# Moving a kernel's key weights and sigmoid weights to other byte offsets in SBUF

## The chip, the core and the metric

The kernel runs on one core of one Trainium2 chip. The metric is device time in microseconds (us), from start to end of one execution. A core has a matrix engine (TensorE; PE in the profile, with its weight loads listed apart as PEld), a vector engine (VectorE, DVE), an activation engine (ScalarE, ACT), a general engine (GpSimd, POOL) and a queue from which all transfers of this kernel start (SP). They run side by side and wait for each other through semaphores. SBUF is the on-chip memory: 128 partitions, each a row of bytes. A tile takes the same byte range in all of them, so a tile has one start address. PSUM is the small memory into which TensorE adds.

## The reference, cut to what matters

The input is x, 256 tokens of 512 numbers, and a context of 25,088 rows of 512. Three layers follow, each added to x. Only the first is touched by the change, and it is most of the work:

```
q = layernorm(x) @ Wq.T + bq            # 256 x 128
k = ctx @ Wk.T + bk                     # 25088 x 128
v = ctx @ Wv.T + bv                     # 25088 x 512
z = sigmoid(q @ k.T / sqrt(128))        # 256 x 25088
x = x + z @ v
```

Then come a causal attention with 16 heads over the 256 tokens, and eight experts of which each token uses one.

## The kernel before, in words

The context is cut into 49 chunks (NCH) of 512 rows (CK). Each chunk is loaded twice, once with the model dimension on the partitions (`rT`) and once with the rows on them (`rN`). Wv isn't applied to the chunks: the kernel adds up z @ ctx in two PSUM banks (`acc`) and applies Wv once at the end.

Products need nearly float32 accuracy. TensorE has a float32r form[...]. So each operand is split into a rounded high part, which ACT writes, and the remainder, a low part, which VectorE or GpSimd computes (`split`, L64 and L65). A product is three matmuls, high by high (L68), high by low (L69) and low by high (L70), all in `mm3`. The first operand is the stationary one (the weights: 128 columns of 4 bytes, 512 bytes in a partition); the second is the moving one (512 columns, 2048 bytes, in most cases). Each matmul has its own weight load, which runs while the matmul ahead of it is streaming.

For a chunk c the loop (it begins at line 263) does:

- `kp_mm`: the key projection. The weights are the four 128-column blocks j of `wk` (high and low tile), the moving data the four blocks of the split, transposed chunk (`T`). 12 matmuls of 512 columns add into one bank; `kp_out` adds bk and splits the keys again (`kp`).
- `scores`: for each half p of the chunk, 6 matmuls of 256 columns; the weights are 128 keys of `kp`, the moving data the split queries `qp`. ACT takes the sigmoid into `z`, VectorE adds it to `zacc` (line 189, for the bias of v), and a split writes the pair `zz[c, p]`. There are four buffers for each part of the pair.
- `av`: the weighted sum. The weights are 128x128 pieces of `zz`, the moving data the four blocks of the split chunk (`N`); for each of two groups of 128 queries 12 matmuls of 512 columns.
- `prepare`: side work that loads other weights, splits them and stores them back to HBM for the last part.

The order of all work on TensorE, ACT, VectorE and GpSimd is the order in which the program is written; `in_order` pins it at the end. Transfers go out in program order on SP.

Addresses come from two pools. The pool `sm` holds small tiles one after another, in the order in which the program first names them, each in a slot rounded up to 32 bytes. The pool `sb` follows it with the large tiles, all of which are multiples of 512 bytes long. A tile with several buffers takes as many slots. `sm` starts at 128 bytes modulo 512. `half`, of which only one column is used, is declared 41 columns wide, and `sb` starts at 0 modulo 512. So the blocks of `wk`, `T`, `kp`, `qp`, `zz` and `N` all start at 0 modulo 512.

At the start, `wk` is split in one piece (ACT and GpSimd); behind it on GpSimd stand the power for the two layer norms (`moments`, L129) and the split of wq. The tiles of `wk` are used again in the last part, as `fr` and `fq` of the experts.

Of the kernel before, what the change touches and what calls it, by code (L numbers as in the profile page):

```python
# [11 lines left out]
F32 = mybir.dt.float32  # L12
F32R = mybir.dt.float32r
BF16 = mybir.dt.bfloat16
# [6 lines left out]
P = 128  # L21
T = 256
D = 512
KD = D // P
# [4 lines left out]
E = 8  # L29
NH = 16  # L30
LAG = 2
# [17 lines left out]
def body(ctx, tc, a, out, nch=NCH):  # L49
    nc = tc.nc  # L50
# [3 lines left out]
    sm = ctx.enter_context(tc.tile_pool(name="sm", bufs=1))  # L54
    sb = ctx.enter_context(tc.tile_pool(name="sb", bufs=1))
# [3 lines left out]
    def f(t):  # L59
        return t.bitcast(F32)  # L60

    def split(hi, lo, src, eng=nc.vector):

        copy(hi, src)  # L64
        eng.tensor_tensor(lo, src, f(hi), ALU.subtract)  # L65

    def mm3(ps, ahi, alo, bhi, blo, first, last):
        mm(ps, lhsT=ahi, rhs=bhi, start=first, stop=False)  # L68
        mm(ps, lhsT=ahi, rhs=blo, start=False, stop=False)  # L69
        mm(ps, lhsT=alo, rhs=bhi, start=False, stop=last)  # L70

    def pair(name, shape, tag=None, bufs=1):
        return [sb.tile(shape, F32R, tag=f"{tag or name}{i}", name=f"{name}_{i}", bufs=bufs) for i in range(2)]

    def bank(name):
        return psum.tile([P, D], F32, tag="b", name=name, bufs=6)
# [4 lines left out]
    def toks(t):  # L81
        return slice(t * P, (t + 1) * P)


    ident = sm.tile([P, P], F32, name="ident")
    make_identity(nc, ident)
    half = sm.tile([P, 41], F32, name="half")[:, 0:1]
    nc.gpsimd.memset(half, -0.5)
    ones = sm.tile([P, 1], F32, name="ones")
    nc.gpsimd.memset(ones, 1.0)  # L90
    x_sb = [sb.tile([P, D], F32, tag=f"x{t}", name=f"x_sb{t}") for t in range(2)]
    bq = sm.tile([P, 1], F32, name="bq")
    bk = sm.tile([P, 1], F32, name="bk")
    bv = sb.tile([P, D], F32, name="bv")
    rows = sm.tile([P, 2], F32, name="rows")
    zacc = sb.tile([P, 2, T], F32, name="zacc")
    nc.vector.memset(zacc, 0.0)
    wv = pair("wv", [P, KD * D], "wvo")
# [1 line left out]


    plain = {"wkvd": D, "wqr": 4 * 64, "wkr": 64, "wku": D, "wvu": D, "wq2": KD * D, "gate": KD * E}
    pw = {n: (sb if w % P == 0 else sm).tile([P, w], F32, name=n) for n, w in plain.items()}
    plain = list(pw)
    spill = {n: dram.tile([P, 2 * w], F32, name=f"sp_{n}") for n, w in (("wo", KD * D), ("gu", E * 2 * D), ("dn", E * D))}

    todo = [("wv", at, None, at) for at in range(0, KD * D, D)]
# [2 lines left out]
    todo += [("wo", at, KD * D, at) for at in range(0, KD * D, D)]  # L110


    mask = sm.tile([P, P], BF16, name="mask")
    nc.gpsimd.memset(mask, 0.0)
    nc.gpsimd.affine_select(out=mask, in_=mask, compare_op=ALU.is_ge, fill=MASKED, base=0, pattern=[[-1, P]],
                            channel_multiplier=1)
# [5 lines left out]
    def moments(x, tag):  # L122
        s6 = sm.tile([P, nc.vector.BN_STATS_DIM], F32, tag="s6", name=f"s6{tag}", bufs=2)
        mv = sm.tile([P, 2], F32, tag="mv", name=f"mv{tag}", bufs=2)
        rs = sm.tile([P, 1], F32, tag="rs", name=f"rs{tag}", bufs=2)
        nc.vector.bn_stats(s6, x)
        nc.vector.bn_aggr(mv, s6)
        nc.vector.tensor_scalar(rs, mv[:, 1:2], 1e-5, None, ALU.add)
        nc.gpsimd.tensor_tensor(rs, rs, half, ALU.pow)  # L129
        return mv, rs  # L130
# [12 lines left out]
    rT, rN, sT, sN, kp, zz = {}, {}, {}, {}, {}, {}  # L143
# [24 lines left out]
    def kp_mm(c, blocks=range(KD)):  # L168
        th, tl = sT[c]
        if c not in kp:  # L170
            kp[c] = bank(f"kp_ps{c}")
        ps = kp[c]
        for j in blocks:
            mm3(ps, wk[0][:, toks(j)], wk[1][:, toks(j)], th[:, j, :], tl[:, j, :], j == 0, j == KD - 1)

    def kp_out(c):
        ps, kp[c] = kp[c], pair(f"kp{c}", [P, CK], "kp", 2)
# [3 lines left out]
    def scores(c, p):  # L181
        ps = bank(f"sc{c}_{p}").rearrange("p (i t) -> p i t", i=2)
        for i in range(2):
            t = toks(2 * p + i)
            mm3(ps[:, i, :], kp[c][0][:, t], kp[c][1][:, t], qp[0], qp[1], True, True)
        z = sb.tile([P, 2, T], F32, tag="z", name=f"z{c}_{p}", bufs=2)
        nc.scalar.activation(z, ps, AF.Sigmoid, scale=1.0 / math.sqrt(128.0))  # L187
        zz[c, p] = pair(f"z{c}_{p}", [P, 2, T], "z", 2 * LAG)
        tt2(zacc, zacc, z, ALU.add)  # L189
        split(*zz[c, p], z)  # L190

# [20 lines left out]
    def load_split(n, tag):  # L212
        r = sb.tile([P, D], F32, tag="wr", name=f"{n}_r", bufs=2)
        nc.sync.dma_start(r, a[n])
        return r, pair(n, [P, D], tag)

    wk_r, wk = load_split("wk", "wk")
    for t in range(2):
        nc.sync.dma_start(x_sb[t], a["x"][:, t, :])
    wq_r, wq = load_split("wq", "at")  # L220
# [8 lines left out]

    acc = [psum.tile([P, D], F32, tag=f"acc{q}", name=f"acc{q}") for q in range(2)]  # L230
    xh, xl = pair("xa", [P, KD, T], "oh")
    warm = sm.tile([P, 1], F32, name="warm")
    nc.scalar.activation(warm, half, AF.Sigmoid)
    split(*wk, wk_r, nc.gpsimd)
    m = [moments(x_sb[tt], f"a{tt}") for tt in range(2)]
    xn = [normal(x_sb[tt], m[tt], f"xa{tt}") for tt in range(2)]
    split(*wq, wq_r, nc.gpsimd)
# [1 line left out]
    for j in range(2):  # L239
        split_T(0, [j])  # L240
        split(xh[:, :, toks(j)], xl[:, :, toks(j)], xps[j])
    split_T(0, [2, 3], nc.gpsimd)
    kp_mm(0, [0, 1])
    qp = pair("qp", [P, T])
    ps = bank("qp_ps")[:, :T]
    for j in range(KD):
        mm3(ps, wq[0][:, toks(j)], wq[1][:, toks(j)], xh[:, j, :], xl[:, j, :], j == 0, j == KD - 1)
    kp_mm(0, [2, 3])
    split_T(1, [0, 1])
    split_T(1, [2, 3], nc.gpsimd)  # L250
    nc.scalar.activation(qp[0], ps, AF.Identity, bias=bq)
    nc.vector.scalar_tensor_tensor(qp[1], ps, bq, f(qp[0]), ALU.add, ALU.subtract)
    kp_out(0)
    split_N(0, [0, 1])
    kp_mm(1, [0, 1])
    scores(0, 0)
    scores(0, 1)
    split_N(0, [2, 3])
    kp_mm(1, [2, 3])
# [3 lines left out]
    for c in range(nch):  # L263
# [23 lines left out]
        for t in range(NT):  # L287
            for q in now:
                av(c, t, q)
            if nx and t in (1, 2):  # L290
                scores(c + 1, t - 1)
        if c >= 4 and plain:
            n = plain.pop()
# [271 lines left out]
    ps = bank("rows_ps")  # L565
# [54 lines left out]
    Q(1, 2)  # L620
    Q(1, 3)
    ft = sb.tile([P, 2 * D], F32R, tag="wq2", name="ft").rearrange("p (n b e d) -> p n b e d", n=2, b=2, e=2)
    fr, fq = (sb.tile([P, 2, 2, P], F32, tag=f"wk{i}", name=f"f{i}") for i in range(2))
    yhl = pair("y", [P, KD, T], "oh")
    PV(0, 2)
    PV(0, 3)
# [144 lines left out]
```

## Time and profile before

| What | Value |
|---|---|
| Median of 2 runs | 585.6 us (585.15 to 586.05) |
| Profiled execution | 586.28 us, its span 584.5 us |
| TensorE matmuls | 570.6 us busy, 98% of the span, 3036 instructions |
| Weight loads | 481.7 us, 82% |
| VectorE, ACT, GpSimd | 79%, 68%, 4% |
| Granted TensorE clock | full |
| DMA | 144.94 MB, mean 248 GB/s |

The span runs from the first to the last instruction; the 1.8 us left over lie around it. "Busy" adds up instructions as the profile shows them. Matmuls are pipelined and overlap, so the mean duration of one (some 390 ns) is longer than the distance between the starts of two, and that distance is the pace. A row of the timeline gives start, length, engine, line, operation, what is written and read, sizes and count. A row of the groups gives count, total busy time, mean, and idle time of the engine ahead of it.

### The profile page before, as it was taken

The numbers are of one execution on the slowest core, as the hardware profiler recorded it, in microseconds if no ns is written. First come the engines' busy times: TensorE is split into PE (matmuls) and PEld (weight loads), VectorE is DVE, ScalarE is ACT, GpSimd is POOL, SyncE is SP. The second block draws the span as 40 slices with busy tenths as digits, with TensorE's granted clock in tenths as the row PEclk, the third lists the DMA queues.
The fourth block names the chain that finished last, engine by engine and source line by source line (L and its number), as shares of the span: only waits on it lengthen the run. The fifth ranks groups of instructions, "written<-read, shape, count | busy, mean of one in ns | idle before, by whom it ended". The sixth has DMA issues, their size and how long they took to land.

```text
span 584.5 us, 8061 instructions
## 1 busy us (share of the span) xinstructions
PE 570.6 (98%) x3036; PEld 481.7 (82%) x3036; DVE 459.7 (79%) x528; ACT 395.1 (68%) x512; POOL 21.1 (4%) x28
## 2 busy tenths in 40 slices
PE   4999999999999999999999999999999999999997
PEld 3888888888888888888888888888888887876996
DVE  6898888888888888888888888787878765667543
ACT  5877777777777777777777776767676752574211
POOL 5200000000000000000000000000000041000000
PEclk9999999999999999999999999999999999999999
DMA  8897887879888888788988887565657477700000
GB/s 288 334 368 283 278 295 281 321 278 317 287 324 276 325 271 325 266 337 298 332 282 319 274 337 245 208 225 206 234 198 243 149 295 262 316 1 1 1 1 36
DMA packets 33526, 144.94 MB, mean 248 GB/s; under 512 B 4240, under 2 KB 4432, under 8 KB 19792
## 3 DMA queue, kind: packets, MB, share of 16 engines
q1 hardware_dynamic: 33488, 144.44, 69.3%
q8 instruction: 23, 0.38, 0.2%
q14 instruction: 15, 0.12, 0.1%
HBM read 129.22 MB, written 15.20 MB: 247 GB/s over the span
## 4 chain that ended last, share of the span: by engine, by line
PE 95%; DVE 3%; DMA 1%; issue 0%; POOL 0%; ACT 0%; SPq 0%; POOLq 0%
PE acc L68 15%; PE acc L69 15%; PE acc L70 15%; PE kp_ps L70 8%; PE kp_ps L69 8%; PE kp_ps L68 8%; PE sc L70 4%; PE sc L69 4%; PE sc L68 4%; PE s L428 2%; PE gu L68 1%; PE gu L69 1%; PE gu L70 1%; PE pt L445 1%; DMA wq_r<-in_wq 1%; PE pv L456 1%
## 5 line engine op out<-in xcount | busy, mean ns | idle before, releaser
L68 PE MATMUL acc<-N,z 128*128 128x512 f32 x392 | 153.9, 393 | 0.0
L69 PE MATMUL acc<-N,z 128*128 128x512 f32 x392 | 153.7, 392 | 0.0
L65 DVE TENSOR_TENSOR N<-rN,N 128x2048 fp32r<-128x2048 f32 (+1 forms) x53 | 111.6, 2110 | 52.3 <-ACT N L64 52.2
L70 PE MATMUL acc<-N,z 128*128 128x512 f32 x392 | 152.5, 389 | 0.0
L65 DVE TENSOR_TENSOR T<-rT,T 128x2048 fp32r<-128x2048 f32 (+1 forms) x49 | 110.3, 2252 | 15.3 <-ACT T L64 15.3
L187 ACT ACTIVATE z<-sc 128x512 f32<-128x512 f32 x98 | 58.7, 599 | 66.5 <-PE sc L70 66.2
L64 ACT CAST N<-rN 128x2048 fp32r<-128x2048 f32 (+1 forms) x55 | 94.4, 1725 | 6.1
L64 ACT CAST T<-rT 128x2048 fp32r<-128x2048 f32 (+1 forms) x55 | 94.3, 1721 | 0.9 <-DMA rT<-in_ctxT 0.7
L70 PEld LDWEIGHTS acc<-N,z 128*128 128x128 f32 x392 | 73.6, 188 | 16.0
L68 PEld LDWEIGHTS acc<-N,z 128*128 128x128 f32 x392 | 74.0, 189 | 12.3
L69 PEld LDWEIGHTS acc<-N,z 128*128 128x128 f32 x392 | 74.0, 189 | 11.7
L68 PE MATMUL kp_ps<-T,wk 128*128 128x512 f32 x196 | 76.9, 392 | 0.0
L70 PE MATMUL kp_ps<-T,wk 128*128 128x512 f32 x196 | 76.7, 392 | 0.0
L69 PE MATMUL kp_ps<-T,wk 128*128 128x512 f32 x192 | 74.7, 389 | 0.0
L189 DVE TENSOR_TENSOR zacc<-zacc,z 128x512 f32<-128x512 f32 x98 | 67.2, 686 | 3.7 <-ACT z L187 1.7
L65 DVE TENSOR_TENSOR z<-z,z 128x512 fp32r<-128x512 f32 x98 | 67.3, 686 | 0.0
L64 ACT CAST z<-z 128x512 fp32r<-128x512 f32 x98 | 61.0, 623 | 3.1
L178 ACT ACTIVATE kp<-kp_ps,bk 128x512 fp32r<-128x512 f32 x49 | 33.9, 691 | 39.9 <-PE kp_ps L70 39.9
L70 PE MATMUL sc<-qp,kp 128*128 128x256 f32 x196 | 55.8, 285 | 0.1
L69 PE MATMUL sc<-qp,kp 128*128 128x256 f32 x196 | 55.4, 283 | 0.0
L68 PE MATMUL sc<-qp,kp 128*128 128x256 f32 x196 | 54.9, 280 | 0.0
L68 PEld LDWEIGHTS kp_ps<-T,wk 128*128 128x128 f32 x196 | 37.1, 189 | 7.8
(177 smaller groups left out, 658.5 us busy)
## 6 DMA issues: line engine op xcount, KB each, us to landing
rN<-in_ctxN SPq DMA_DIRECT2D x49, 1024.0 KB, 5.7
rT<-in_ctxT SPq DMA_DIRECT2D x47, 1024.0 KB, 5.5
sp_gu<-w_gu SPq DMA_DIRECT2D x32, 256.0 KB, 4.3
gu<-sp_gu SPq DMA_DIRECT2D x8, 1024.0 KB, 6.0
r_gu<-in_gu SPq DMA_DIRECT2D x16, 256.0 KB, 5.7
sp_dn<-w_dn SPq DMA_DIRECT2D x16, 256.0 KB, 4.3
dn<-sp_dn SPq DMA_DIRECT2D x16, 256.0 KB, 6.0
r_dn<-in_dn SPq DMA_DIRECT2D x8, 256.0 KB, 6.1
```

The costliest lines, as they stand in the source:

```text
L64: copy(hi, src)
L65: eng.tensor_tensor(lo, src, f(hi), ALU.subtract)
L68: mm(ps, lhsT=ahi, rhs=bhi, start=first, stop=False)
L69: mm(ps, lhsT=ahi, rhs=blo, start=False, stop=False)
L70: mm(ps, lhsT=alo, rhs=bhi, start=False, stop=last)
L178: nc.scalar.activation(kp[c][0], ps, AF.Identity, bias=bk)
L187: nc.scalar.activation(z, ps, AF.Sigmoid, scale=1.0 / math.sqrt(128.0))
L189: tt2(zacc, zacc, z, ALU.add)
L428: mm(p3[:, h - h0:h - h0 + 2, :], lhsT=qs[:, tt, h // 2, g, :], rhs=kbd[g // 2][:, g % 2, h:h + 2, :nk], start=tt == 1, stop=tt == 0 and h ...
L445: nc.tensor.transpose(ps[:, toks(i * (tt + 1) + kt)], pr[tt, u][:, i, toks(kt)], ident)
L456: mm(pv[tt][r, g, :], lhsT=vs[kt][:, g * P + r.start:g * P + r.stop], rhs=pt[tt, u][:, toks(i * (tt + 1) + kt)], start=kt == 0, stop=kt == tt)
```

## The change: what it does

`wk`'s two tiles move from `sb` to `sm` and become 16 columns longer. The four blocks are no longer adjacent: they begin at columns 1, 132, 264 and 400. The declarations of small tiles are reordered, `half` becomes 16 columns wide and a `pad` of 8 columns is added, so that both tiles of `wk` and the pool `sb` start at 32 modulo 512. The split of `wk` goes block by block: four casts and four subtractions in place of one each. Each buffer of `zz` becomes 16 columns (64 bytes) longer, of which the data use the first 512. `fr` and `fq` take their place in the longer `wk` tiles.

```
+    wkp = [None, None]
+    wkp[0] = sm.tile([P, D + 16], F32R, tag="wk0", name="wk0")
+    plain = {"wkr": 64, "gate": KD * E}
+    pw = {n: sm.tile([P, w], F32, name=n) for n, w in plain.items()}
+    half = sm.tile([P, 16], F32, name="half")[:, 0:1]
+    wkp[1] = sm.tile([P, D + 16], F32R, tag="wk1", name="wk1")
+    pad = sm.tile([P, 8], F32, name="pad")
     ident = sm.tile([P, P], F32, name="ident")
-    half = sm.tile([P, 41], F32, name="half")[:, 0:1]
...
-            mm3(ps, wk[0][:, toks(j)], wk[1][:, toks(j)], th[:, j, :], tl[:, j, :], j == 0, j == KD - 1)
+            mm3(ps, wk[0][j], wk[1][j], th[:, j, :], tl[:, j, :], j == 0, j == KD - 1)
...
-        zz[c, p] = pair(f"z{c}_{p}", [P, 2, T], "z", 2 * LAG)
+        zz[c, p] = [t[:, 0:2 * T].rearrange("p (i t) -> p i t", i=2)
+                    for t in pair(f"z{c}_{p}", [P, 2 * T + 16], "z", 2 * LAG)]
...
-    wk_r, wk = load_split("wk", "wk")
+    wk_r = sb.tile([P, D], F32, tag="wr", name="wk_r", bufs=2)
+    nc.sync.dma_start(wk_r, a["wk"])
+    wk = [[t[:, o:o + P] for o in (1, 132, 264, 400)] for t in wkp]
...
-    split(*wk, wk_r, nc.gpsimd)
+    for j in range(KD):
+        split(wk[0][j], wk[1][j], wk_r[:, toks(j)], nc.gpsimd)
...
-    fr, fq = (sb.tile([P, 2, 2, P], F32, tag=f"wk{i}", name=f"f{i}") for i in range(2))
+    fr, fq = (sm.tile([P, D + 16], F32, tag=f"wk{i}", name=f"f{i}")[:, 0:D].rearrange("p (b e d) -> p b e d", b=2, e=2)
+              for i in range(2))
```

More of the change, by code (lines that the diff above doesn't have):

```diff
@@ L82, in toks @@
         return slice(t * P, (t + 1) * P)
+    ones, bq, bk, warm = [sm.tile([P, 1], F32, name=n) for n in ("ones", "bq", "bk", "warm")]
+    rows = sm.tile([P, 2], F32, name="rows")
+    mask = sm.tile([P, P], BF16, name="mask")
+    wkp = [None, None]
[5 more added lines that the diff above has]
+    pad = sm.tile([P, 8], F32, name="pad")
     ident = sm.tile([P, P], F32, name="ident")
     make_identity(nc, ident)
-    half = sm.tile([P, 41], F32, name="half")[:, 0:1]
     nc.gpsimd.memset(half, -0.5)
-    ones = sm.tile([P, 1], F32, name="ones")
     nc.gpsimd.memset(ones, 1.0)
     x_sb = [sb.tile([P, D], F32, tag=f"x{t}", name=f"x_sb{t}") for t in range(2)]
-    bq = sm.tile([P, 1], F32, name="bq")
-    bk = sm.tile([P, 1], F32, name="bk")
     bv = sb.tile([P, D], F32, name="bv")
-    rows = sm.tile([P, 2], F32, name="rows")
     zacc = sb.tile([P, 2, T], F32, name="zacc")
@@ L102, in body @@
     plain = {"wkvd": D, "wqr": 4 * 64, "wkr": 64, "wku": D, "wvu": D, "wq2": KD * D, "gate": KD * E}
-    pw = {n: (sb if w % P == 0 else sm).tile([P, w], F32, name=n) for n, w in plain.items()}
-    plain = list(pw)
+    pw.update({n: (sb if w % P == 0 else sm).tile([P, w], F32, name=n) for n, w in plain.items() if n not in pw})
+    plain = list(plain)
     spill = {n: dram.tile([P, 2 * w], F32, name=f"sp_{n}") for n, w in (("wo", KD * D), ("gu", E * 2 * D), ("dn", E * D))}
@@ L110, in body @@
     todo += [("wo", at, KD * D, at) for at in range(0, KD * D, D)]
-    mask = sm.tile([P, P], BF16, name="mask")
     nc.gpsimd.memset(mask, 0.0)
@@ L231, in body @@
     xh, xl = pair("xa", [P, KD, T], "oh")
-    warm = sm.tile([P, 1], F32, name="warm")
     nc.scalar.activation(warm, half, AF.Sigmoid)
-    split(*wk, wk_r, nc.gpsimd)
+    for j in range(KD):
+        split(wk[0][j], wk[1][j], wk_r[:, toks(j)], nc.gpsimd)
     m = [moments(x_sb[tt], f"a{tt}") for tt in range(2)]
```

## The prediction

> **What bounds the kernel now.** I read the page's busy times and its chain of work first, then the groups of TensorE, then the timeline of one chunk, then a table of stretches.
>
> ```profile
> PE 570.6 (98%) x3036; PEld 481.7 (82%) x3036; DVE 459.7 (79%) x528; ACT 395.1 (68%) x512; POOL 21.1 (4%) x28
> ...
> PE 95%; DVE 3%; DMA 1%; issue 0%; POOL 0%; ACT 0%; SPq 0%; POOLq 0%
> ...
> L68 PE MATMUL acc<-N,z 128*128 128x512 f32 x392 | 153.9, 393 | 0.0
> ...
> L70 PE MATMUL acc<-N,z 128*128 128x512 f32 x392 | 152.5, 389 | 0.0
> ...
> L68 PE MATMUL kp_ps<-T,wk 128*128 128x512 f32 x196 | 76.9, 392 | 0.0
> ```
>
> TensorE is 95% of the chain and idle before none of these groups, so only the pace of matmuls counts. The mean of 390 ns is no pace, because matmuls overlap; the pace is the distance between starts. These rows are PE's timeline around the key projection and then around scores:
>
> ```profile
> 211.38 0.39 PE L68 MATMUL kp_ps<-T,wk 128*128 128x512 f32 x1
> 211.61 0.39 PE L69 MATMUL kp_ps<-T,wk 128*128 128x512 f32 x1
> ...
> 214.10 0.39 PE L68 MATMUL acc<-N,z 128*128 128x512 f32 x1
> ...
> 216.93 0.28 PE L69 MATMUL sc<-qp,kp 128*128 128x256 f32 x1
> ...
> 217.53 0.40 PE L68 MATMUL acc<-N,z 128*128 128x512 f32 x1
> ...
> 218.69 0.39 PE L70 MATMUL acc<-N,z 128*128 128x512 f32 x1
> ```
>
> From 211.38 to 214.10 twelve projections start: 2.72/12 = 226.7 ns each. From 216.93 to 217.53 five score matmuls of 256 columns start: 120 ns each. After scores the weighted sum is a little slower: 217.53 to 218.69 holds five, 232 ns each. Now an uncomplicated float32 product of the tail and, from the table of stretches, ten microseconds with the loads going and ten with none:
>
> ```profile
> 521.17 1.02 PE L428 MATMUL s<-kbd,qs 128*128 128x512 f32 x2
> 522.03 0.27 PE L431 MATMUL s<-mask,identb 128*128 128x256 bf16 x1
> ...
> 200.00:210.00 10.00, 10.00 (x54) 8.55 (x53) 8.62 (x10) 7.36 (x8) 0.00 (x0) 1.00 0.87 301
> 546.00:556.00 10.00, 10.00 (x69) 9.14 (x68) 6.34 (x20) 1.80 (x5) 0.55 (x1) 1.00 0.00 0
> ```
>
> The pair at 521.17 occupies 0.86 us, 430 ns an instruction. If each streams its 512 columns twice (float32 shows two instructions per product here[...]), that is 215 ns a pass. So a float32r matmul of 512 columns pays about 11 ns that a float32 pass does not. Clock and busy share are full both with DMA at 0.87 and at 0.00 (the columns before the last), so neither throttle nor transfers make the 11 ns.[...]
>
> [...]
>
> **The change part by part.** *Layout.* Before, all large buffers lie at 0 modulo 512, since their sizes are multiples of 512 and the small pool ends on one. So every weight block and its moving operand are 0 apart. After, small tiles come in 32-byte slots from 128 modulo 512: four of 32, rows 32, mask 256, and wk0 starts at 544, that is 32. Its 2112 bytes, wkr 256, gate 128 and half 64 make 2560, so wk1 is at 32 too. Then 2112, pad 32 and 1440 of others make 3584 = 7 x 512, and the large pool starts at 32. Block starts of 4, 528, 1056 and 1600 bytes are 4, 16, 32 and 64 past the keys. The eight sigmoid buffers of 2112 bytes step by 64: high halves 0 to 192, low halves 256 to 448. So one of four high buffers stays at 0; as two of three loads are of high halves, that is 1176 x 2/3 x 1/4 = 196 of the weighted sums below. Scores (kp against qp) stay 0 apart.
>
> *What it touches.* 3 x 4 x 49 = 588 projections and 3 x 392 = 1176 weighted sums: 1764 matmuls, 1764 x 226.7 = 399.9 us of the span. Each nanosecond of mean pace is 1.76 us, so 2% of the run (11.7 us) is 6.6 ns. Of the 1764, 1568 get a new distance. The 588 score matmuls (70.6 us) keep theirs. In the tail some expert down-projections see other distances, 48 matmuls at most: 0.5 us if all 11 ns vanish.
>
> *What a distance costs.* The trace has no float32r matmul at a distance other than 0. Lower bound of the pace: the float32 pass, 215.7, a gain of 11 x 1568 = 17.2 us. Upper bound: a weight load of 128 columns takes 188 ns and one of 64 takes 137, so reading 128 takes about 2 x 51 = 102 ns (estimate). If the moving stream is held to half speed for all of it, it loses 51 ns instead of 11: +40 x 1568 = +63 us. I take **zero**. The 11 ns is the same at 512 columns (226.7 - 215.7) and at 256[...], with keys, context rows and queries as moving data from unrelated buffers: a fixed toll per load of float32r weights fits as well as any conflict of addresses. Both streams also travel far in 102 ns: 512 bytes of weights, about twice that of moving data (2048 bytes in 215 ns). A starting distance of 4 to 64 bytes is passed in a few ns[...].
>
> *Four pieces for the split of wk.* ACT's cast of 512 columns takes 0.62 us; four of 128 take 0.62 to 2.5 in all. ACT starts at 3.37 and has nothing until 7.17 (wq_r lands), so even 2.5 hides. POOL is tighter:
>
> ```profile
> 4.07 1.26 POOL L65 TENSOR_TENSOR wk<-wk_r,wk 128x512 fp32r<-128x512 f32 x1 [2.08 <-ACT wk L64]
> 5.34 0.55 POOL L129 TENSOR_TENSOR rsa<-rsa,half 128x1 f32<-128x1 f32 x1
> 7.20 0.79 POOL L129 TENSOR_TENSOR rsa<-rsa,half 128x1 f32<-128x1 f32 x1 [1.31 <-DMA wq_r<-in_wq]
> ```
>
> Behind the pieces wait the first power (5.34), the second (7.20) and the split of wq, and behind the powers the normalisation and transposes of x. Four pieces cost 1.26 to 5.04 us. On a line through 0.55 (one column) and 1.26 (512), a piece is 0.73, so 2.9. They can start at about 3.7, after the first short cast, end at 6.6, and the first power at 7.2. VectorE wants it at 7.04. Delay 0.2 us, bounds 0 and 2.3. DMAs, their order and every wait of the chunk loop stay; nothing else of the change issues an instruction. [...]
>
> *Sum.* Profiled execution 586.3 (span 584.5 plus 1.8 around it) + 0.2 = 586.5. The median of the two runs is 585.6, 0.7 below the profiled one; so **586** on the scale of the runs.
>
> **The rivals.** *Slower: the moving stream runs into the weights.* Place: the 980 weighted sums with a new distance, of 64 to 448 bytes. If the moving stream, twice as fast, cannot pass a line that the weights hold, it trails behind them for the rest of the load and loses half a nanosecond per nanosecond. A start at 0 keeps it ahead for most of the load (11 ns lost); for distances spread over 512 the meeting falls anywhere, and the mean loss is half of 51, 25 ns. Over the 11 lost now that is +14.5 x 980 = 14 us: **600**. With the projections as well, + 8.5, it is 609. It decides once the mean pace of all 1764 passes 226.7, and costs over 2% from 233 on. For it: paces of 232 after scores[...], so the toll isn't rigid, and all such deviations are upward. Against: the pace falls back to 226.7 by itself in six matmuls[...].
>
> *Faster: equal addresses are the conflict.*[...] All 1568 matmuls at 215.7 give 586 - 17.2 = **569**; if only 64 bytes and more help, 980 and 147 matmuls, 12.4 us, 574. For it: the toll is absent where the moving data run at half rate or the weights are bfloat16. Against:[...] no row shows a better distance.
>
> *The layout isn't what it says* (slots rounded otherwise): distances shift, most remain nonzero, and the same three outcomes hold, so it gets no number of its own.
>
> **How the numbers follow.** No effect of distance: 0.56, 586, own range 584 to 590. Slower rival, full or partial (partial: the 232 ns seen after scores everywhere, +5 x 1568 = 8 us, 594): 0.27. Faster rival, full or partial (half of these, 577): 0.17. About 2% is what a measurement of this kernel can tell from no change. Of the slower chance 0.21 lies over 597.3 and 0.06 below; of the faster 0.12 under 573.9 and 0.05 above it. So faster 0.12, same 0.67, slower 0.21. The range runs from just over the faster rival's 569 to 603, between the slower's 600 and 609, leaving about 0.07 below and 0.12 above.
>
> **What would show it.** PE's timeline of a chunk: twelve projections, three per block, and 24 weighted sums. Starts at 227 ns for all four blocks and all buffers prove the forecast; 216 in some blocks the faster rival; over 233 in chunks that use particular sigmoid buffers the slower one, and the distance can be read off since blocks and buffers each have their own. Scores must keep 120. POOL's four pieces should end before 7.0 us and the first projection start near 10.3. The forecast is wrong if a few ns of pace depend on distance at all, since 1764 matmuls multiply them.

## The result and the profile after

The changed kernel took 592.07 us, the median of 2 runs (591.79 to 592.35), against 585.6 before: a ratio of 1.011 (95% interval 1.0067 to 1.0154). It is slower by 6.5 us, inside the range given and within 2%, but it isn't the "no effect" that was forecast as likeliest: it lies outside the 584 to 590 given for that case. With two runs of each kernel the interval leaves 3.9 to 9.0 us for the difference. The profiled execution has a span of 589.7 us in place of 584.5, so 5.2 us are there to be found in the traces.

The page of the changed kernel: busy times, clock by slices, chain by engine, three groups of TensorE.

```profile
PE 575.7 (98%) x3036; PEld 481.2 (82%) x3036; DVE 459.8 (78%) x528; ACT 395.2 (67%) x515; POOL 21.5 (4%) x31
...
PEclk9999999999999999999999999999999999999999
...
PE 95%; DVE 2%; DMA 1%; POOL 0%; SPq 0%; issue 0%; ACT 0%; POOLq 0%
...
L70 PE MATMUL acc<-N,z 128*128 128x512 f32 x392 | 154.4, 394 | 0.0
...
L70 PE MATMUL kp_ps<-T,wk 128*128 128x512 f32 x196 | 77.8, 397 | 0.0
L68 PE MATMUL kp_ps<-T,wk 128*128 128x512 f32 x196 | 77.7, 396 | 0.0
```

TensorE does the same 3036 matmuls, never idle in front of these groups, at full clock, and is busy 5.1 us longer (575.7 less 570.6). VectorE, ACT, the weight loads and the transfers are as before. So matmuls follow each other more slowly. In a table of stretches, the same 300 us of both kernels hold 1495 and then 1480 matmuls (the count behind PE; first row before, then after, at the same full clock):

```profile
100.00:400.00 300.00, 300.00 (x1495) 254.82 (x1494) 254.37 (x246) 226.86 (x243) 0.00 (x0) 1.00 0.82 289
```

```profile
100.00:400.00 300.00, 300.00 (x1480) 251.94 (x1479) 252.20 (x243) 224.31 (x243) 0.00 (x0) 1.00 0.81 288
```

PE's timeline of one chunk of the changed kernel, projections and the first sums behind them:

```profile
213.49 0.40 PE L68 MATMUL kp_ps<-T,wk 128*128 128x512 f32 x1
...
214.19 0.39 PE L68 MATMUL kp_ps<-T,wk 128*128 128x512 f32 x1
...
214.88 0.39 PE L68 MATMUL kp_ps<-T,wk 128*128 128x512 f32 x1
...
215.57 0.39 PE L68 MATMUL kp_ps<-T,wk 128*128 128x512 f32 x1
...
216.27 0.40 PE L68 MATMUL acc<-N,z 128*128 128x512 f32 x1
...
218.34 0.39 PE L68 MATMUL acc<-N,z 128*128 128x512 f32 x1
...
219.02 0.28 PE L68 MATMUL sc<-qp,kp 128*128 128x256 f32 x1
```

Twelve projections take 216.27 - 213.49 = 2.78 us (2.72 before), 232 ns each; the three of each block take 0.69 to 0.70 us in place of 0.68. Behind them nine weighted sums take 2.07 us, 230 ns each, and the last three 0.68, 227 ns each: the old pace comes back in the pair of sigmoid buffers that lies at 0 and 256.

From all distances between starts in the two traces: the mean pace of a projection went from 226.8 to 231.4 ns, which over 588 is 2.7 us; that of a weighted sum from 228.9 to 231.3 ns, over 1176 2.8 us. Scores went from 119.8 to 119.4 ns, -0.2 us. Together that is 5.3 us, and the spans differ by 5.2.

### The profile page after: what moved, and what is told of

Read it like the earlier page. It is cut to its first block, busy times and chain, and to the rows that moved or that the text cites. A ratio compares the mean times of both kernels' runs of the same rounds, so it can differ in the third digit from the quotient of the medians.

```text
span 589.7 us, 8067 instructions
## 1 busy us (share of the span) xinstructions
PE 575.7 (98%) x3036; PEld 481.2 (82%) x3036; DVE 459.8 (78%) x528; ACT 395.2 (67%) x515; POOL 21.5 (4%) x31
## 4 chain that ended last, share of the span: by engine, by line
PE 95%; DVE 2%; DMA 1%; POOL 0%; SPq 0%; issue 0%; ACT 0%; POOLq 0%
PE acc L70 15%; PE acc L68 15%; PE acc L69 15%; PE kp_ps L70 8%; PE kp_ps L68 8%; PE kp_ps L69 8%; PE sc L70 4%; PE sc L68 4%; PE sc L69 4%; PE s L437 2%; PE gu L68 1%; PE gu L70 1%; PE gu L69 1%; PE pt L454 1%; DMA wq_r<-in_wq 1%; PE pv L465 1%
## 5 line engine op out<-in xcount | busy, mean ns | idle before, releaser
L70 PE MATMUL kp_ps<-T,wk 128*128 128x512 f32 x196 | 77.8, 397 | 0.0
L68 PE MATMUL kp_ps<-T,wk 128*128 128x512 f32 x196 | 77.7, 396 | 0.0
L69 PE MATMUL kp_ps<-T,wk 128*128 128x512 f32 x192 | 75.2, 392 | 0.0
```

## The experiments

Each run was timed beside the kernel before on the same chip; e1 to e4, e5 to e8 and e9 to e12 each shared one chip and its runs of the kernel before. "Pace" is the mean distance between starts over all projections or all weighted sums of its trace, without the 9 to 11 distances of 300 ns and more that each trace has, nearly all at the start and the end. "Distance" is where the next weights start, counted from the start of the moving data, modulo 512 bytes.

| Run | Distance of key blocks / sigmoid buffers, bytes | us (before beside it) | Ratio, 95% interval | Pace of projections, sums, ns |
|---|---|---|---|---|
| before | 0 / 0 | | | 226.8, 228.9 |
| change | 4, 16, 32, 64 / 0 to 448 | 592.07 (585.6) | 1.0067 to 1.0154 | 231.4, 231.3 |
| e1 | 0 / 0 | 586.85 (586.41) | 0.9999 to 1.0017 | 226.8, 228.9 |
| e2 | 4, 16, 32, 64 / 0 | 592.14 (586.41) | 1.0089 to 1.0116 | 233.3, 230.6 |
| e3 | 0 / 0 to 448 | 589.73 (586.41) | 1.0046 to 1.0071 | 228.1, 230.8 |
| e4 | 64 / 0 | 591.56 (586.41) | 1.0080 to 1.0106 | 233.2, 230.1 |
| e5 | 16 / 0 | 586.03 (586.05) | 0.9992 to 1.0009 | 226.9, 229.0 |
| e6 | -16 / 0 | 586.29 (586.05) | 0.9995 to 1.0012 | 226.8, 229.0 |
| e7 | 256 / 0 | 586.58 (586.05) | 0.9998 to 1.0016 | 226.7, 228.9 |
| e8 | 128 / 0 | 591.67 (586.05) | 1.0079 to 1.0109 | 232.9, 230.4 |
| e9 | 32 / 0 | 590.32 (586.11) | 1.0043 to 1.0087 | 232.8, 229.5 |
| e10 | 4 / 0 | 590.35 (586.11) | 1.0052 to 1.0088 | 231.7, 230.3 |
| e11 | 4, 16, 32, 16 / 0 | 591.43 (586.11) | 1.0073 to 1.0108 | 232.8, 230.8 |
| e12 | 0 / 0, queries moved by 64 | 585.96 (586.11) | 0.9989 to 1.0008 | 227.1, 228.9 |

**e1: everything of the change but the distances.** Edit against the changed kernel:

```
-    wk = [[t[:, o:o + P] for o in (1, 132, 264, 400)] for t in wkp]
+    wk = [[t[:, o:o + P] for o in (0, 128, 256, 384)] for t in wkp]
...
-        zz[c, p] = [t[:, 0:2 * T].rearrange("p (i t) -> p i t", i=2)
-                    for t in pair(f"z{c}_{p}", [P, 2 * T + 16], "z", 2 * LAG)]
+        zz[c, p] = pair(f"z{c}_{p}", [P, 2, T], "z", 2 * LAG)
```

> The change with all distances put back to 0: the key blocks adjacent and at the start of their tiles, the sigmoid buffers 2048 bytes long. What stays is the large pool at 32 modulo 512 and the split of wk in four pieces. Distance theory (the slower pace comes from the distances alone): 585.9, the old pace of 226.7 ns in projections and sums, and 0.25 us for a later first projection. Placement theory (operands at 32 modulo 512, or the split, cost the time): 592, pace about 231 ns.

586.85 against 586.41, and both paces are those of the kernel before. The pool at 32 modulo 512 and the split in four pieces together cost less than the 0.2% that the interval allows. The placement theory is out.

**e2 and e3: one half each.** e2 is the changed kernel with the second edit of e1 alone, e3 with the first alone.

> Key blocks at 4, 16, 32, 64 as in the change, sigmoid buffers back to 0. Distance theory: the projections stay at 231.4 ns on average (+2.7 us), weighted sums are back near 228.9 except the first ones behind a projection: 588.5 to 589. Placement theory: 592.

> Sigmoid buffers 64 bytes apart as in the change, key blocks back to 0. Distance theory: sums at 231.3 ns on average (+2.8 us), projections back at 227: 588.5 to 589. Placement theory: 592. If the two parts add up, the gains of this run and of the one with the keys alone sum to 6 us.

Each half alone is slower, so each contributes. The 592 of e2 is also what the placement theory asked for, but e1 has taken that one out. The two halves don't add up: worked out from the paces (their changes times 588 and 1176), e2 loses 5.8 us and e3 3.0, and both together lose 5.5. The expectation that they would was a miss, and e2 alone is as slow as the whole. In e2 the projections run at 233.3 ns, though the same four distances gave 231.4 in the changed kernel, and the sums, all at distance 0, lose 1.7 ns. In e3 the projections, at distance 0, lose 1.3 ns. So a matmul's pace depends on what came before it, and not on its own distance alone. In e2's timeline the projections, the first sums behind them, and the last three ahead of the scores:

```profile
214.01 0.39 PE L68 MATMUL kp_ps<-T,wk 128*128 128x512 f32 x1
...
216.81 0.40 PE L68 MATMUL acc<-N,z 128*128 128x512 f32 x1
217.04 0.39 PE L69 MATMUL acc<-N,z 128*128 128x512 f32 x1
217.27 0.39 PE L70 MATMUL acc<-N,z 128*128 128x512 f32 x1
217.50 0.40 PE L68 MATMUL acc<-N,z 128*128 128x512 f32 x1
...
218.88 0.39 PE L68 MATMUL acc<-N,z 128*128 128x512 f32 x1
...
219.56 0.28 PE L68 MATMUL sc<-qp,kp 128*128 128x256 f32 x1
```

2.80 us for twelve projections; then sums at distance 0 that start 230 ns apart on average from 216.81 to 217.50 (0.69 us for three), and 227 from 218.88 to 219.56 (0.68 for three). To the nanosecond the distances of these sums are 236, 224, 231, 236, 228, 233, 230 and then 227: seven matmuls until the old pace is back. In the kernel before, the sums behind scores come back in nearly the same steps (233, 236, 228, 233, 231, 226).

**e4: one distance for all key blocks.** Offsets (16, 144, 272, 400), buffers as in e1.

> All four key blocks 64 bytes past the keys, sigmoid buffers at 0. Distance theory (each distance has a pace of its own): 233 ns in all 588 projections, as the block at 64 showed, +3.7 us: 589.5. Switching theory (what costs is that the distance changes from block to block, and a uniform distance settles again): the projections return to 227 after the first few, 586 to 586.5.

The switching theory falls: with one and the same distance the projections don't come to rest in the twelve of a chunk. The first starts of one chunk in e4:

```profile
213.29 0.40 PE L68 MATMUL kp_ps<-T,wk 128*128 128x512 f32 x1
213.53 0.39 PE L69 MATMUL kp_ps<-T,wk 128*128 128x512 f32 x1
213.76 0.40 PE L70 MATMUL kp_ps<-T,wk 128*128 128x512 f32 x1
214.00 0.39 PE L68 MATMUL kp_ps<-T,wk 128*128 128x512 f32 x1
...
216.09 0.39 PE L68 MATMUL acc<-N,z 128*128 128x512 f32 x1
```

The trace has these starts to the nanosecond, and there they alternate: 236, 231, 236, 231, 235, 231. Twelve take 2.80 us. The time, 5.2 us more, beats the 3.7 expected of the projections alone by what the sums behind them lose: 1.2 ns x 1176 = 1.4 us.

**e5 to e10: which distances.** e5, e9 and e10 change the offsets alone: (4, 132, 260, 388), (8, 136, 264, 392), (1, 129, 257, 385), buffers as in e1. e6 to e8 move the large pool under the key tiles instead, by a wider pad; e6:

```
-    pad = sm.tile([P, 8], F32, name="pad")
+    pad = sm.tile([P, 16], F32, name="pad")
...
+    wk = [[t[:, o:o + P] for o in (4, 132, 260, 388)] for t in wkp]
```

The pad is 72 columns in e7 and 104 in e8, with offsets (0, 128, 256, 384), so the pool starts at 288 and at 416.

> All four key blocks 16 bytes past the keys, everything else 0 apart. Settling theory (a pace near 226.7 is a state of its own that only some distances reach; at 64 it is never reached and the pace swings between 231 and 236): if 16 is one that reaches it, as three matmuls of the changed kernel hint (227, 226), 587; if not, 233 ns as at 64 and 591.5. Size theory (the toll grows with the distance, 16 is a quarter of 64): pace about 228.5, 588.

> All key blocks 16 bytes ahead of the keys (496 past modulo 512), everything else 0 apart. Chase theory (moving data trail behind weights that lie a little past them): weights that lie behind cost less than at 0, pace under 226.7, 584 or less. Settling theory: 227 or 233, nothing between, so 587 or 591.5. Size theory, by the shorter way round: as at +16.

> All key blocks 256 bytes past the keys, half of the assumed period. In the run with the sigmoid buffers alone, the buffer pair at 0 and 256 kept the pace of 226.7. If the pattern repeats after 256 bytes: 226.7 in the projections and 586.5 to 587. If it repeats after 512 alone and the low half at 256 was carried by the high half at 0: 233 and 591.5. Chase theory: the meeting falls in the middle of the load, the mean loss of 25 ns, 240 ns and more than 594.

> All key blocks 128 bytes past the keys, everything else 0 apart. Sigmoid buffers at 128 with 384 paced 228 to 241 ns, mean 233. Settling theory: 232 to 234 in the projections, 591. If the pattern repeats after 128 bytes: 226.7 and 587. Chase theory: worse than at 256.

> All key blocks 32 bytes past the keys, everything else 0 apart. Settling theory: so far 0, 16 past, 16 before and 256 settle at 226.7 ns, 64 and 128 swing around 233. 32 lies between; it has to give one of the two, 586 or 591.5, and not the 588.5 of a toll that grows with the distance.

> All key blocks 4 bytes past the keys, the only distance that is no multiple of 16 bytes. Settling theory, with 0 and 16 on either side settled: 226.7 ns and 586. [...]

There are two classes and little between them. At 0, 16, -16 and 256 the projections settle at 226.7 to 226.9 ns, and the kernel's time can't be told from before. At 4, 32, 64 and 128 they run at 231.7 to 233.2 and it is 4.2 to 5.6 us slower. e7 next to e4 above, twelve projections in 2.72 us:

```profile
211.44 0.39 PE L68 MATMUL kp_ps<-T,wk 128*128 128x512 f32 x1
...
214.16 0.39 PE L68 MATMUL acc<-N,z 128*128 128x512 f32 x1
```

The chase theory falls with e6 (no gain with the weights behind: 226.8 ns) and e7 (no loss at half the assumed period: 226.7 ns, where it asked for 240 and more). The size theory falls with e10 against e7: 4 bytes cost 4.2 us, 256 none. For e10 the settling theory missed: 4 lies between two harmless distances, 0 and 16, and isn't one; it costs 4.9 ns (231.7 less 226.8). "Settled" is a name for the 227 ns; no run shows what lies behind it.

One rival has no run of its own: that the address of the weights matters by itself, and not the distance from the moving data. e8 answers it. The key tiles begin at 32 modulo 512 in e1, e7 and e8 alike, and the projections take 226.8, 226.7 and 232.9 ns. Nor is the place of the data at fault, 416 in e8: sums whose weights and data both lie there come back to 227 ns.

How long the coming back takes depends on the distance left behind. In e9 (32) the sums behind the projections are at the old pace after one matmul; eleven of them take 2.49 us, 226 ns each:

```profile
215.13 0.39 PE L68 MATMUL acc<-N,z 128*128 128x512 f32 x1
215.36 0.39 PE L69 MATMUL acc<-N,z 128*128 128x512 f32 x1
...
217.85 0.28 PE L68 MATMUL sc<-qp,kp 128*128 128x256 f32 x1
```

In e10 (4) it takes five, in e4 (64) six, in e8 (128) seven and in e11 below eight.

**e11: without the block at 64.** Offsets (1, 132, 264, 388), buffers as in e1. Four columns of the fourth block overwrite the end of the third, so its keys are not the reference's; all instructions and their number are the same.

> The key blocks of the change, but the fourth at 16 in place of 64; sigmoid buffers at 0. With the fourth at 64 this was 592.1, with 233.3 ns in the projections. If the block at 64 alone throws the others off their pace: 226.7 to 228 and 586 to 587. If a change of distance from block to block does it, whatever the distances: 231 or more and 590 to 592.

591.43 us, 5.3 more than the kernel before beside it, where e2 with the block at 64 took 5.7 more: the block at 64 isn't alone. The two blocks at 16, harmless when all are at 16, run at 233.4 ns here between neighbours at 4 and 32. Since 4 and 32 are unsettled distances themselves, the run doesn't tell whether the switching adds anything. In e3 a pair of buffers at 0 and 256, which switches at two of three loads but between settled distances, held 226.8 and 226.9 ns.

**e12: a try for a gain.** Edit against the kernel before:

```
+    sb.tile([P, 16], F32, name="padq")
     qp = pair("qp", [P, T])
+    sb.tile([P, 112], F32, name="padq2")
```

> The kernel before, with the split queries moved 64 bytes on, so that the score weights lie 64 bytes ahead of them; projections and sums stay 0 apart. In the kernel before the six weighted sums after each group of scores take 1.39 us in place of 1.36, some 2.7 us in all. If the scores leave TensorE in a phase that their own distance sets, the six sums change: to 583 at best, if the loss is gone. If the scores are bound by their weight loads (120 ns for 256 columns), their own pace stays at 120, and with an unchanged phase after them 586.

No gain (ratio 0.9989 to 1.0008). Scores stay at 119.5 ns. The six sums behind the first group of scores get another pattern, 241, 224, 231, 236, 228, 232 ns in one chunk in place of 233, 236, 228, 233, 231, 226, with nearly the same sum (1.39 us). Those behind the second begin with 230, 224 and take 1.38 us, and the first projection behind them takes 231 ns in place of 227. No run here beats the kernel before.

## Why the prediction was right, and where it was wrong

The time lies in the range and the change is under 2%, but not for the reason given. The case that carried the forecast, no effect of distance, did not happen, and the prediction's own sign of being wrong did: a few nanoseconds of pace depend on distance. That the change stayed under 2% was luck of size. The mean pace of the 1764 matmuls rose by 3.1 ns (4.6 x 588 and 2.4 x 1176), where 6.6 make 2%, and the range held 592 because it had been stretched over the slower rival.

**Bound and weight of the pace: right.** TensorE's pace was the only thing that counted. For each of e1 to e12, (change of the projections' pace) x 588 + (change of the sums' pace) x 1176 gives the change of time within 0.5 us: for e8, 6.1 x 0.588 + 1.5 x 1.176 = 5.4 us against 5.6 measured; for e9 3.5 + 0.7 = 4.2 against 4.2.

**Layout: right, as far as the paces show it.** Blocks and buffers at different distances behaved differently, the pair at 0 and 256 kept the old pace (226.8 and 226.9 ns in e3), and scores kept 120 ns.

**"What a distance costs: I take zero": wrong.** This step failed: it is +4.6 ns in the projections and +2.4 ns in the sums, part of it in matmuls at distance 0 that follow others. Two arguments carried the zero. The first was that a toll of 11 ns at 512 and at 256 columns, with unrelated buffers, is a fixed toll of the load. The 215 ns behind it, half of the 430 ns of a float32 instruction, was an estimate, and bfloat16 matmuls of the kernel before bear it out: behind one of 512 columns the next starts after 216 ns (L426, all four), behind one of 256 after 109 to 110 (L431, six of eight), where float32r takes 226.7 and 119.8. Six float32r matmuls between 547.87 and 549.23, at a DMA share of 0.00, also start 227 ns apart. But the buffers of keys, context rows and queries all lay at the same distance, 0, so the sample couldn't show a dependence; the remaining 11 ns may still be fixed, as no distance lowered them (226.7 ns at the least, e7). The second was an estimate, that a starting distance of 4 to 64 bytes is passed in a few ns. Being short, it doesn't make a distance harmless: in e4 against e5 48 bytes decide between 233.2 and 226.9 ns.

**"The pace falls back to 226.7 by itself": right, but not at every distance.** At distance 0 the pace comes back within one to eight matmuls, and at 16, -16 and 256 it stays (226.7 to 226.9 ns). At 64 it doesn't come back within twelve (233.2 ns, e4). What brings it back is not shown.

**The slower rival: the partial case by size, not by mechanism.** The case "232 ns everywhere", 594, is close to what happened (231.4 and 231.3 ns, 592.07), and it had the smaller chance. Its full form, a moving stream that trails behind the weights and loses 25 ns, is refuted by e6 and e7 (226.8 and 226.7 ns). Its evidence, the 232 ns after scores, was the right row to look at: it showed that the toll isn't rigid, and its steps are those that e2's sums take behind the projections.

**The faster rival: refuted.** Equal addresses aren't the conflict. No settled group runs faster than at distance 0 (226.7 to 226.9 ns against 226.8), although single matmuls of 224 ns occur (in e2 and e12).

**The four pieces: mis-sized, harmless.** POOL of the changed kernel at the start:

```profile
3.81 1.65 POOL L65 TENSOR_TENSOR wk<-wk_r,wk 128x128 fp32r<-128x128 f32 x4 [1.82 <-ACT wk L64]
5.44 0.55 POOL L133 TENSOR_TENSOR rsa<-rsa,half 128x1 f32<-128x1 f32 x1
```

They took 1.65 us and not 2.9, 0.41 each; the line through the power's 0.55 us was a poor one, as that power of one column took longer than a subtraction of 128 columns. The first power starts 0.1 us later and isn't waited for. The first projection starts at 10.58 in place of 10.33, but this start lies between 9.86 and 10.93 in the runs here, so the profile gives no cost to the pieces.

**Weights and moving data: not independent here.** Where the weights lie relative to the moving data changes the matmul's pace by up to 6.4 ns (226.8 to 233.2, e4). By what means, no run shows. Multiples of 16 bytes stand in both classes: 16 and 256 at 226.9 and 226.7 ns, 32, 64 and 128 at 232.8, 233.2 and 232.9.

**What stays open.** Why 0, 16, -16 and 256 settle and 4, 32, 64 and 128 don't, whether the pattern repeats after 512 bytes or less, and whether 192 and 448 belong to either class. The distances were tested in the projections alone, one by one; for the weighted sums only in mixtures. One of these mixtures is a hint: in e3 the six sums behind the first scores of a chunk whose buffers lie at 192 and 448 take 1.37 us on average, where the same six take 1.39 at 0. Over the 24 such chunks that is an estimated 0.4 us, and e3 as a whole is slower than the kernel before.

## What to carry to other kernels

A pace that is the same in many matmuls shows nothing about a parameter that is the same in all of them; before taking its effect as zero, ask whether the sample varies it at all. When TensorE is the bound, compare distances between starts group by group and look for groups that swing; here 3 ns on each of some 1800 matmuls were 1% of the kernel. Padding that moves weights against moving data can change the pace (4 bytes cost 4.2 us here, 16 cost nothing that the runs can tell), and here leaving both at the same offset was as good as any that was tried.

## What the runs showed of the hardware

- The projections, float32r matmuls of 512 columns with a weight load each, start 226.7 to 226.9 ns apart when the next weights lie 0, 16, -16 or 256 bytes past the moving data modulo 512, and 231.7 to 233.2 ns at 4, 32, 64 and 128 (e1, e4 to e10).
- The pace depends on what ran before. After an unsettled group, matmuls at distance 0 need from one (e9) to eight (e11) to come back to 226.7 ns, and the costs of two such changes don't add up (by the paces 5.8 and 3.0 us alone, 5.5 together).
- Matmuls of 256 columns at 120 ns hardly react at the one other distance tried (119.8 before, 119.5 with the queries moved by 64, e12).
- The start of the operands against a multiple of 512, when all move together, made no difference that the runs can tell (32: ratio 0.9999 to 1.0017, e1; with the keys at a settled distance also 64: 0.9995 to 1.0012, e6, and 288: 0.9998 to 1.0016, e7).
